# A transformer block on one core: an earlier start, reordered products and moved small work in the attention turns

## Chip, cores and metric

The kernel runs on 1 core of one Trainium2 chip. The metric is the device time of one execution in microseconds. Before the change it is 1411.21 us, the median of 3 runs (1409.51 to 1415.54).

## What is computed

Eight sequences of 512 tokens and 256 features, 16 heads of 16, go through two residual blocks. Everything is float32. Cut to its core, with `ln` for a layer norm without weights and `rn` for an RMS norm:

```python
def attn_block(x):                       # first block, applied to ln(x)
    q, k, v = split(x @ Wqkv_w.T + Wqkv_b)
    ctx = causal_attn(q, k, v)
    q2 = conv1d(ctx, conv_w, width=3, padding=1) + conv_b
    ctx2 = causal_attn(q2, k, v)         # the same k and v again
    return ctx2 @ out_w.T + out_b

def ffn_block(x):                        # second block, applied to ln(x)
    h = x + causal_attn_rotary(rn(x) @ wq, rn(x) @ wk, rn(x) @ wv) @ wo
    t = rn(h)
    w = top2_of_softmax(t @ w_router)    # 8 experts, two per token, weights scaled to sum 1
    return h + sum_over_experts(w * ((silu(t @ wg) * (t @ wu)) @ wd))

x = x + attn_block(ln(x))
x = x + ffn_block(ln(x))
```

So each sequence needs three causal attentions: one with q, one with q2, one with rotary q and k.

## The kernel before

**Two stages.** The first some 870 us are the attentions of all eight sequences and all that lies between them. Then come the experts, which gather their tokens from a table in DRAM (`xtab`) and are a plain row of matmuls. A sequence is a `Batch`; sequences go in pairs, and `one` and `two` are the pair at work, `before0` and `before1` the pair before it, `next0` and `next1` the next. The three attentions of a pair alternate between its two members.

**Steps and turns.** An attention of one sequence is 9 steps. A step computes, for one or two blocks of 64 keys, scores in two PSUM buffers `sc` (L1290) and an exponential out of each (L1297, ScalarE). GpSimd then masks the diagonal (L1305). The products with V (L1220) follow some steps later. A turn is two steps, a pair of sequences takes 27 turns, and there are 108 turns in all. Turn t+2 below is the third turn of a pair of sequences: turns 29, 56 and 83 for the second to fourth pair (turns 0 to 4 have a list of their own). In the profile turn 29 begins at 239.11 us and turn 30 at 248.09 us. The loop at the end of the kernel writes out each turn in this order:

1. first scores and their two exponentials
2. products with V of earlier steps (`catch_up`)
3. follow-ups listed as "mid"
4. `small_units[n]`, then `first_units[n]`
5. second scores and their two exponentials
6. follow-ups "late", then `units[n]`, then follow-ups "end"

Units are all other work of a sequence: projections, transposes, norms, routing. `plan(turn, batch, what, ...)` puts a unit into `units`, or into the list named with `among`. The block runs under `manual_schedule`, so PE, ScalarE, VectorE and GpSimd each execute their instructions in the order in which the program writes them. SP sends most DMAs.

**Resources.** `mm_tile()` hands out two PSUM banks in turn; a product that takes a bank waits until whoever read the product before last from that bank is done. The scores have two buffers, so a step's scores wait for the exponentials of the step before.

**Lines that the change and the prediction touch.**
- `load_x` (L746): one DMA of 512 KB for a sequence. `wqkv_sb` (L927) and `bqk_sb` (L944) are the QKV weights and the column of q and k biases. `bk_sb` (L1043) needs that column and `parity`.
- `stats` (L1385): mean and variance of each of four token chunks on VectorE (L1113, L1114), plus epsilon (L1391), power of -1/2 on GpSimd (L1392). `normed` (L1397) applies them (L1400). `transpose` turns the result by PE (L1372) and copies it out of PSUM on VectorE or ScalarE (L1376). `q`, `k`, `values` are projections (L1130, L1148) with their copies (L1436 q, L1419 k, L1166 values).
- `table_inputs` and `table`: the rotary tables, turned by PE (L1095) and copied by ScalarE (L1097), once.
- `normalise` (called when the products with V of half an attention are complete) copies sums out of PSUM (L1237, ScalarE), moves them by DMA (`r`, `cs`), and lists `finish` (L1250, L1251, VectorE) and `then`, which is `differences` in the first attention (four VectorE operations, L1471 to L1474) for the later `conv`.
- `bias`: one GpSimd addition to x for a chunk. `x1`: the residual after the first block and the norms behind it.
- `route`: some 25 small VectorE operations and one ScalarE exponential (L1675 to L1692). `slots`: two small products (L1706, L1707), some 20 small VectorE operations, then indirect DMAs from GpSimd (L1730) sent one by one in later turns.
- `h` (L1616 on): the output projection of the rotary attention for half of the tokens (PE L1119), the sum (VectorE L1622), the sum into x (GpSimd L1623), and the squares (ScalarE L1625), whose element-wise output goes back into the PSUM bank and whose row sums are what is used. `rms` follows both halves: L1632 (VectorE), L1633 (GpSimd), L1636 (VectorE).

At the start the program does 34 transposes of the identity into PSUM (L1906), whose result nobody reads.

Of the kernel before, what the change touches and what calls it, by code (L numbers as in the profile page):

```python
# [11 lines left out]
F32 = mybir.dt.float32  # L12
I32 = mybir.dt.int32
AF = mybir.ActivationFunctionType
# [677 lines left out]
def fast_path(  # L692
# [52 lines left out]

    def load_x(b):  # L746
        if b < B:
            xs[b] = keep.tile([P, NC, D], F32, tag="x", name="x", bufs=4)
            nc.sync.dma_start(xs[b], x[b * S : (b + 1) * S, :].rearrange("(c p) d -> p c d", p=P))

# [11 lines left out]

    load_x(0)

# [157 lines left out]
    with ExitStack() as att:  # L922
# [31 lines left out]
        for i in range(1, 3):  # L954
            va.append(wp.tile([P, NB, PAIRS, HP], F32, tag=f"va{i}", name=f"va{i}"))

        wqkv_sb = weight(wqkvT, 3 * D, "wqkv_sb")
        bqk_sb = column(bqkv[: 2 * D], 2 * D, "bqk_sb")
        nc.gpsimd.dma_start(bv_sb, bqkv[2 * D :].partition_broadcast(P))
# [52 lines left out]
        for i, n in enumerate((N, 2 * N, CAP + N)):  # L1012
# [25 lines left out]
            turns, ident.rearrange("p (f i) -> p i f", i=2), AX.X, ALU.add  # L1038
        )

        bk_sb = wp.tile([P, DC, 2], F32, tag="bk", name="bk_sb")
        for ch in range(DC):
            nc.vector.tensor_scalar(  # L1043
                bk_sb[:, ch, :], parity, bqk_sb[:, DC + ch : DC + ch + 1], None, ALU.mult
            )

# [157 lines left out]
        def attention(qT, kT, v, to, then=None):  # L1204
# [25 lines left out]
            def normalise(ch):  # L1230
# [28 lines left out]
                if then is not None:  # L1259
                    follow(1 - ch, lambda: then(ch), where)  # L1260
                follow(3 - 2 * ch, check, "late")
# [71 lines left out]
        class Batch:  # L1333
# [50 lines left out]

            def stats(self):  # L1385
                self.xb = xs.pop(self.b)
                mv = self.mv = small.tile([P, NC, 2], F32, tag="mv", name="mv")
                for c in range(NC):
                    moments(mv, self.xb, c)
                rstd = self.rstd = small.tile([P, NC], F32, tag="rstd", name="rstd")  # L1390
                nc.vector.tensor_scalar(rstd, mv[:, :, 1], LN_EPS, None, ALU.add)  # L1391
                nc.gpsimd.tensor_tensor(rstd, rstd, neghalf[:, 0, :], ALU.pow)  # L1392

            def fetch_next(self):
                load_x(self.b + 1)

            def normed(self):  # L1397
                xn = self.xn = self.normed_tile("xn")
                for c in range(NC):
                    nc.vector.tensor_scalar(  # L1400
                        xn[:, c, :],
                        self.xb[:, c, :],
                        self.mv[:, c, 0:1],
                        self.rstd[:, c : c + 1],
                        ALU.subtract,
                        ALU.mult,
                    )
                self.xT = self.tile([P, DC, S], "xT", "xT")

# [206 lines left out]
            def h(self, half):  # L1616
                if half == 0:
                    self.ss = small.tile([P, NC], F32, tag="ss", name="ss")
                two = slice(2 * half, 2 * half + 2)
                ps = self.project_two(self.c3, wo_sb, half)  # L1620
                h = self.rows[:, two, :D]
                nc.vector.tensor_add(h, h, ps)  # L1622
                nc.gpsimd.tensor_tensor(self.xb[:, two, :], self.xb[:, two, :], h, ALU.add)  # L1623
                for c in range(2 * half, 2 * half + 2):
                    nc.scalar.activation(  # L1625
                        ps[:, c - 2 * half], self.rows[:, c, :D], AF.Square, accum_out=self.ss[:, c : c + 1]
                    )
# [145 lines left out]
        for p in range(B // 2 + 1):  # L1773
# [5 lines left out]
            plan(t, before0, "transpose3", (0, True), (1, True))  # L1779
            plan(t, two, "q", 0)  # L1780
            plan(t, before0, "logits")
# [4 lines left out]
            plan(t + 1, before1, "normed2", 2, 3)  # L1786
            plan(t + 2, before1, "h", 0, 1)
            plan(t + 2, before1, "rms")
            plan(t + 3, two, "q", 1, among=first_units)
            plan(t + 3, two, "k", 1)  # L1790
            plan(t + 3, before0, "slots")
            plan(t + 3, next0, "fetch_next")
# [15 lines left out]
            plan(t + 11, next0, "k", 0)  # L1808
            for c in range(NC):
# [88 lines left out]
        with tc.manual_schedule(  # L1898
# [224 lines left out]
```

## Time and profile before

| what | value |
|---|---|
| median of the runs | 1411.21 us |
| profiled execution, its time | 1413.67 us |
| its span, first to last instruction | 1411.9 us |
| VectorE, ScalarE, GpSimd busy | 52%, 51%, 37% of the span |
| mean granted PE clock | 0.994 |
| exponentials (L1297) | 432 of 1023 ns |
| a projection matmul of q or k (L1130, 128x512) | 624 ns |
| load of x, 512 KB, from issue to landing | 4.3 us |
| load of the QKV weights, 768 KB | 6.1 us |
| load of the bias column, 2 KB | 7.5 us |

PE is TensorE's matmuls, PEld its weight loads, DVE VectorE, ACT ScalarE, POOL GpSimd, SP the engine that issues DMAs. In an order of time, a line gives the start and the length in us, the engine, the line of the program, the operation, what it writes and reads, and how many instructions were merged. A bracket gives the idle time of the engine before it and who ended it.

### The profile page before, as it was taken

Reading aid. Unit: us, or ns where it says so; the run is one execution under the profiler, and the core shown is the slowest. Engines: PE = TensorE matmul, PEld = TensorE weight load, DVE = VectorE, ACT = ScalarE, POOL = GpSimd, SP = SyncE. Lnnn points to the kernel's source line nnn. Section 1 sums busy time; section 2 is a strip of 40 time slices with the busy share of each in tenths; the row PEclk is TensorE's granted clock in tenths of the full one; section 3 lists DMA queues with packets and bytes.
Section 4 is the critical chain, followed back from the end, with each engine's and each line's share of the span. In section 5 each row is a group of like instructions: output and inputs, shape, how many; then the busy total and the mean of one; then the engine's idle time right before and its main releaser. Section 6 shows DMA issues by size and latency. Waiting matters only on the chain.

```text
span 1411.9 us, 31919 instructions
## 1 busy us (share of the span) xinstructions
PE 1369.0 (97%) x13476; PEld 892.3 (63%) x13476; DVE 739.6 (52%) x1470; ACT 723.6 (51%) x1175; POOL 525.2 (37%) x525
## 2 busy tenths in 40 slices
PE   8999999999999899999999999999999999999997
PEld 5566555566555566556565566666767677776775
DVE  5754886775887665886666865322222212222221
ACT  4677777776786677777776784321111211111120
POOL 3334434547333546433555444232122121222212
PEclk9999999999999999999999999999999999999998
DMA  5122122211001211011222022334141323232311
GB/s 151 59 82 86 66 82 77 73 40 62 13 25 53 73 40 55 20 45 39 83 72 79 21 84 71 90 81 102 23 102 31 96 32 95 46 87 42 88 26 14
DMA packets 66408, 88.42 MB, mean 63 GB/s; under 512 B 12752, under 2 KB 46736, under 8 KB 66256
## 3 DMA queue, kind: packets, MB, share of 16 engines
q1 hardware_dynamic: 52976, 68.94, 14.7%
q0 software_dynamic: 13280, 17.35, 7.0%
q8 instruction: 107, 1.75, 0.5%
q14 instruction: 45, 0.37, 0.1%
HBM read 36.35 MB, written 31.82 MB: 48 GB/s over the span
## 4 chain that ended last, share of the span: by engine, by line
PE 59%; DVE 5%; ACT 4%; DMA 1%; issue 1%; POOL 1%; DVEq 0%; POOLq 0%; ACTq 0%; SPq 0%
PE pgu L835 23%; PE po L860 13%; PE sc L1290 8%; PE av L1220 5%; PE mm L1130 3%; ACT pr L1297 2%; PE mm L1483 2%; PE mm L1119 1%; PE mm L1148 1%; PE mm L824 1%; DVE r L1250 1%; DVE c L1251 1%; PE mm L1372 1%; DMA r<-cs 1%; DMA cs<-cs 0%
## 5 line engine op out<-in xcount | busy, mean ns | idle before, releaser
L1297 ACT ACTIVATE pr<-sc 128x1024 f32<-128x1024 f32 x432 | 418.8, 1023 | 145.1 <-PE sc L1290 144.6
L1305 POOL TENSOR_TENSOR pr<-pr,seen 128x512 f32<-128x512 f32 (+1 forms) x216 | 256.6, 1188 | 395.7 <-ACT pr L1297 386.2
L835 PE MATMUL pgu<-xgT,gu 128*128 128x384 f32 (+1 forms) x1056 | 337.0, 478 | 1.9 <-DVE hT L850 1.6
L835 PEld LDWEIGHTS pgu<-xgT,gu 128*128 128x128 f32 x1056 | 200.4, 190 | 128.3 <-DVE hT L850 2.2
L849 ACT ACTIVATE sg<-pgu 128x384 f32<-128x384 f32 (+1 forms) x120 | 57.7, 481 | 404.5 <-PE pgu L835 404.4
L872 POOL DMA_INDIRECT out_dram<-share,xg x72 | 111.0, 1542 | 373.8 <-DVE share L867 299.6
L1220 PE MATMUL av<-pr,va 64*32 64x512 f32 (+7 forms) x6144 | 216.3, 407 | 0.0
L1290 PE MATMUL sc<-qT,kT 32*128 32x320 f32 (+7 forms) x2048 | 192.2, 436 | 4.3 <-ACT pr L1297 4.2
L850 DVE TENSOR_TENSOR hT<-sg,pgu 128x384 f32<-128x384 f32 (+1 forms) x120 | 65.0, 543 | 240.3 <-ACT sg L849 240.3
L860 PE MATMUL po<-dn,hT 128*128 128x256 f32 (+1 forms) x864 | 190.8, 379 | 0.0
L1220 PEld LDWEIGHTS av<-pr,va 64*32 64x32 f32 x6144 | 112.1, 106 | 101.2 <-issue 73.5
L860 PEld LDWEIGHTS po<-dn,hT 128*128 128x128 f32 (+1 forms) x864 | 159.9, 187 | 23.9
L1250 DVE RECIPROCAL r<-r 128x256 f32<-128x256 f32 x96 | 167.4, 1744 | 11.8 <-DMA r<-cs 11.7
L1290 PEld LDWEIGHTS sc<-qT,kT 32*128 32x128 f32 x2048 | 115.7, 185 | 78.3 <-ACT pr L1297 32.0
L867 DVE TENSOR_SCALAR share<-po,xg 128x256 f32<-128x256 f32 (+1 forms) x72 | 34.8, 483 | 148.6 <-PE po L860 148.5
L1290 PE MATMUL sc<-q2T,kT 32*128 32x512 f32 (+7 forms) x1024 | 93.0, 434 | 0.6 <-ACT pr L1297 0.5
L1730 POOL DMA_INDIRECT xtab<-rows,slot x64 | 64.0, 1000 | 46.0 <-DVE pick L1719 29.0
L1290 PEld LDWEIGHTS sc<-q2T,kT 32*128 32x128 f32 x1024 | 58.3, 184 | 32.7 <-issue 14.5
L1130 PE MATMUL mm<-xT,wqkv_sb 128*128 128x512 f32 x128 | 63.7, 624 | 3.9 <-ACT mm L1625 2.3
L1130 PE MATMUL mm<-xaT,wqkv_sb 128*128 128x512 f32 x128 | 61.3, 612 | 2.0 <-DVE xaT L1378 2.0
L1483 PE MATMUL mm<-terms,conv_sb 128*128 128x256 f32 x256 | 62.7, 390 | 0.0
L1237 ACT ACTIVATE cs<-av 128x512 f32<-128x512 f32 x96 | 56.6, 604 | 3.7 <-PE av L1220 3.2
(181 smaller groups left out, 1305.5 us busy)
## 6 DMA issues: line engine op xcount, KB each, us to landing
r<-cs SPq DMA_DIRECT2D x96, 128.0 KB, 2.0
xtab<-pad SPq DMA_DIRECT2D x24, 397.5 KB, 3.3
xg<-xtab SPq DMA_DIRECT2D x16, 397.5 KB, 3.0
gu<-in_wg_dram SPq DMA_DIRECT2D x18, 352.0 KB, 3.1
cs<-cs SPq DMA_DIRECT2D x48, 128.0 KB, 2.0
dn<-in_wd_dram SPq DMA_DIRECT2D x9, 640.0 KB, 5.1
gu<-in_wu_dram SPq DMA_DIRECT2D x18, 320.0 KB, 3.8
x<-in_x_dram SPq DMA_DIRECT2D x8, 512.0 KB, 4.3
```

The costliest lines, as they stand in the source:

```text
L835: nc.tensor.matmul(ps, gu[d][:, n0 : n0 + P], xgT[:, d, :], start=(d == 0), stop=(d == DC - 1),)
L850: nc.vector.tensor_mul(hT[k], sg, pu)
L860: nc.tensor.matmul(po, hT[k][:, s * P : s * P + m], dn[:, k, :], start=(k == 0), stop=(k == NK - 1),)
L872: nc.gpsimd.indirect_dma_start(out=out, out_offset=token_of(xg, s, m), in_=share[:m, s, :], in_offset=None, bounds_check=B * S - 1, oob_is ...
L1130: nc.tensor.matmul(ps, w[:, d, n0 : n0 + P], srcT[:, d, :S], start=(d == 0), stop=(d == DC - 1),)
L1220: nc.tensor.matmul(av[i][g * HP : (g + 1) * HP, j * KB :], v[rows, j, ch * G + g, :], pr[rows, g, at : at + n], start=(j == 0), stop=(j == ...
L1250: nc.vector.reciprocal(r[:, half], r[:, half])
L1290: nc.tensor.matmul(sc[:, g - g0, at : at + S - j * KB], kT[r0 : r0 + HP, ch, j], qT[r0 : r0 + HP, ch, j * KB : S], start=True, stop=True,)
L1297: nc.scalar.activation(pr[:, g0 : g0 + 2], sc, AF.Exp, scale=SCALE)
L1305: nc.gpsimd.tensor_tensor(diag, diag, seen.unsqueeze(1).unsqueeze(1).to_broadcast([P, G, len(parts), KB]), ALU.mult,).ins
L1483: nc.tensor.matmul(ps[:, i], conv_sb[:, d, k, ch * P : (ch + 1) * P], self.terms[d][:, k], start=(d == 0), stop=(d == DC - 1),)
L1730: nc.gpsimd.indirect_dma_start(out=xtab, out_offset=bass.IndirectOffsetOnAxis(ap=slot[:, c, k : k + 1], axis=0), in_=rows[:, c, :], in_off ...
```

## The change

- The first sequence's x is loaded as two DMAs; its moments, power and normalisation go by halves. The bias column is loaded ahead of the QKV weights, and `bk_sb` is computed behind the normalisation instead of ahead of it. The first sequence's transposes go by halves of the tokens, with one copy on ScalarE and one on VectorE. 22 transposes of the identity instead of 34.
- `then` (the differences) always goes to the "end" list.
- The squares in `h` are written to an SBUF tile (`t1`, which two other places also use) instead of the PSUM bank.
- `q` of `two` in turn t, the first half of `h` of `before1` in turn t+2, `slots` of `before0` in turn t+3, and `next1`'s transposes in turn t+25 go from `units` to `first_units`, ahead of the turn's second scores.
- The bias additions go to turns 6, 8, 10, 11 (`one`) and 10, 11, 15, 15 (`two`), instead of 10 to 13 and 14 to 17.
- The four rotary `table` units go from turns 3, 3, 4, 4 (`units`) to turns 2, 3, 4, 5 (`small_units`).

```diff
-    def load_x(b):
+    def load_x(b, parts=1):
...
-            nc.sync.dma_start(xs[b], x[b * S : (b + 1) * S, :].rearrange("(c p) d -> p c d", p=P))
+            of = x[b * S : (b + 1) * S, :].rearrange("(c p) d -> p c d", p=P)
+            n = NC // parts
+            for c in range(0, NC, n):
+                nc.sync.dma_start(xs[b][:, c : c + n, :], of[:, c : c + n, :])
...
-    load_x(0)
+    load_x(0, 2)
...
+        bqk_sb = column(bqkv[: 2 * D], 2 * D, "bqk_sb")
         wqkv_sb = weight(wqkvT, 3 * D, "wqkv_sb")
-        bqk_sb = column(bqkv[: 2 * D], 2 * D, "bqk_sb")
...
-        for ch in range(DC):
-            nc.vector.tensor_scalar(
-                bk_sb[:, ch, :], parity, bqk_sb[:, DC + ch : DC + ch + 1], None, ALU.mult
-            )
+        def bias_by_parity():
+            for ch in range(DC):
+                nc.vector.tensor_scalar(
+                    bk_sb[:, ch, :], parity, bqk_sb[:, DC + ch : DC + ch + 1], None, ALU.mult
+                )
...
                 if then is not None:
-                    follow(1 - ch, lambda: then(ch), where)
+                    follow(1 - ch, lambda: then(ch), "end")
...
+            def transpose_halves(self):
+                ps = [mm_tile() for _ in range(DC)]
+                for half in range(2):
+                    for d in range(DC):
+                        for c in range(2 * half, 2 * half + 2):
+                            nc.tensor.transpose(
+                                ps[d][:, c * P : (c + 1) * P],
+                                self.xn[:, c, d * P : (d + 1) * P],
+                                ident,
+                            )
+                for d in range(DC):
+                    (nc.scalar.copy, nc.vector.tensor_copy)[d](self.xT[:, d, :S], ps[d])
...
+                squares = small.tile([P, S], F32, tag="t1", name="t1", bufs=2)
                 for c in range(2 * half, 2 * half + 2):
                     nc.scalar.activation(
-                        ps[:, c - 2 * half], self.rows[:, c, :D], AF.Square, accum_out=self.ss[:, c : c + 1]
+                        squares[:, :D], self.rows[:, c, :D], AF.Square, accum_out=self.ss[:, c : c + 1]
                     )
...
-            plan(t, two, "q", 0)
+            plan(t, two, "q", 0, among=first_units)
...
-            plan(t + 2, before1, "h", 0, 1)
+            plan(t + 2, before1, "h", 0, among=first_units)
+            plan(t + 2, before1, "h", 1)
...
-            plan(t + 3, before0, "slots")
+            plan(t + 3, before0, "slots", among=first_units)
...
-            for c in range(NC):
-                plan(t + 10 + c, one, "bias", c)
-                plan(t + 14 + c, two, "bias", c)
+            for c, n in enumerate((6, 8, 10, 11)):
+                plan(t + n, one, "bias", c)
+            for c, n in enumerate((10, 11, 15, 15)):
+                plan(t + n, two, "bias", c)
...
-                plan(t + 25, next1, "transpose", (0, True), (1, True))
+                plan(t + 25, next1, "transpose", (0, True), (1, True), among=first_units)
...
-            units[3 + n // 2].append(lambda n=n: table(n))
+            small_units[2 + n].append(lambda n=n: table(n))
...
-                for i in range(17):
+                for i in range(11):
...
-            one.stats()
-            one.normed()
+            one.stats(0, 2)
+            one.stats(2, 2)
+            one.normed(0, 2)
+            one.normed(2, 2)
+            bias_by_parity()
+            one.transpose_halves()
             two.stats()
-            one.transpose(0)
-            one.transpose(1)
```

`stats(first, n)` and `normed(first, n)` do what they did, for n chunks from the first on.

More of the change, by code (lines that the diff above doesn't have):

```diff
@@ L1382, in transposed, with stats, normed @@
                     nc.scalar.mul(to[:, d, :S], ps, scale[:, d : d + 1])
-            def stats(self):
-                self.xb = xs.pop(self.b)
-                mv = self.mv = small.tile([P, NC, 2], F32, tag="mv", name="mv")
-                for c in range(NC):
[L1389 to L1392, printed above, removed]
+            def stats(self, first=0, n=NC):
+                if first == 0:
+                    self.xb = xs.pop(self.b)
+                    self.mv = small.tile([P, NC, 2], F32, tag="mv", name="mv")
+                    self.rstd = small.tile([P, NC], F32, tag="rstd", name="rstd")
+                some = slice(first, first + n)
+                for c in range(first, first + n):
+                    moments(self.mv, self.xb, c)
+                rstd = self.rstd[:, some]
+                nc.vector.tensor_scalar(rstd, self.mv[:, some, 1], LN_EPS, None, ALU.add)
+                nc.gpsimd.tensor_tensor(rstd, rstd, neghalf[:, 0, some], ALU.pow)
             def fetch_next(self):
                 load_x(self.b + 1)
-            def normed(self):
-                xn = self.xn = self.normed_tile("xn")
-                for c in range(NC):
+            def normed(self, first=0, n=NC):
+                if first == 0:
+                    self.xn = self.normed_tile("xn")
+                    self.xT = self.tile([P, DC, S], "xT", "xT")
+                xn = self.xn
+                for c in range(first, first + n):
                     nc.vector.tensor_scalar(
@@ L1407, in normed @@
                     )
-                self.xT = self.tile([P, DC, S], "xT", "xT")
+            def transpose_halves(self):
[10 more added lines that the diff above has]
+                    (nc.scalar.copy, nc.vector.tensor_copy)[d](self.xT[:, d, :S], ps[d])
             def transpose(self, d, soon=False):
@@ L1808, in fast_path @@
             plan(t + 11, next0, "k", 0)
-            for c in range(NC):
-                plan(t + 10 + c, one, "bias", c)
-                plan(t + 14 + c, two, "bias", c)
+            for c, n in enumerate((6, 8, 10, 11)):
+                plan(t + n, one, "bias", c)
+            for c, n in enumerate((10, 11, 15, 15)):
+                plan(t + n, two, "bias", c)
             plan(t + 12, two, "conv", (0, 0), among=first_units)
```

## The prediction

> **What bounds the kernel now.** I read the page first, then PE's waits, then the order of time on single engines around the places that the diff touches. Times below are those of the profiled execution (span 1411.9 us, run 1413.67 us, 2.5 us above the median of 1411.21 us).
>
> ```profile
> PE 1369.0 (97%) x13476; PEld 892.3 (63%) x13476; DVE 739.6 (52%) x1470; ACT 723.6 (51%) x1175; POOL 525.2 (37%) x525
> PE 59%; DVE 5%; ACT 4%; DMA 1%; issue 1%; POOL 1%; DVEq 0%; POOLq 0%; ACTq 0%; SPq 0%
> ```
>
> PE works 97% of the span, and the change takes no matmul away except 12 warm-up transposes. All it can win is PE's idle time, and only before 870 us: the experts behind that are PE without gaps. PE's waits (us in total, times, longest):
>
> ```profile
> PE sc L1290 <- ACT pr L1297: 4.7, 9, 0.9
> PE mm L1372 <- DVE va L1166: 4.5, 2, 2.8
> PE mm L1130 <- ACT mm L1625: 2.3, 3, 0.9
> PE mm L1095 <- ACT kT L1419: 1.3, 1, 1.3
> PE mm L1095 <- DVE va L1166: 1.2, 1, 1.2
> ```
>
> Each is a place that the diff edits: scores that wait for an exponential, transposes that wait for a PSUM bank which VectorE or ScalarE still reads. One of them costs more than its length. Here are windows of 1 us after the 2.85 us gap of turn 59 (columns: PE, PEld, DVE, ACT, POOL busy, clock, DMA share, GB/s):
>
> ```profile
> 478.00:479.00 1.00, 0.00 (x0) 0.00 (x0) 1.00 (x3) 1.00 (x4) 0.93 (x1) 1.00 0.00 0
> 479.00:480.00 1.00, 0.12 (x1) 0.15 (x2) 0.72 (x2) 0.13 (x2) 0.84 (x2) 0.51 0.28 109
> 484.00:485.00 1.00, 1.00 (x2) 0.48 (x3) 0.91 (x3) 1.00 (x2) 0.00 (x0) 0.50 0.00 0
> 486.00:487.00 1.00, 1.00 (x6) 0.29 (x8) 0.96 (x2) 0.18 (x1) 0.95 (x1) 1.00 0.00 0
> ```
>
> The granted clock fell to half from about 479.5 to 485.6. The same work (transposes to the next values) took 487.80 - 479.88 = 7.92 us here and 274.69 - 269.37 = 5.32 us in turn 32, so the gap cost 2.85 + 2.6.
>
> **The start.** PE's first useful work was released by this chain on VectorE:
>
> ```profile
> 5.20 0.43 DVE L1113 BATCH_NORM_STATS2 st<-x 128x6 f32<-128x256 f32 x1 [2.13 <-DMA x<-in_x_dram]
> 7.46 0.17 DVE L1391 TENSOR_SCALAR rstd<-mv 128x4 f32<-128x4 f32 x1
> 9.46 0.36 DVE L1043 TENSOR_SCALAR bk_sb<-parity,bqk_sb 128x2 f32<-128x2 f32 x2 [1.45 <-DMA bqk_sb<-in_bqkv_dram]
> 9.73 1.38 DVE L1400 TENSOR_SCALAR xn<-x,mv,rstd 128x256 f32<-128x256 f32 x4
> 12.16 0.43 DVE L1113 BATCH_NORM_STATS2 st<-x 128x6 f32<-128x256 f32 x1 [1.05 <-DMA x<-in_x_dram]
> ```
>
> The pow (POOL, 7.71 to 8.76) was done 0.7 us before the bias column, behind which the normalisation was queued. The change takes the column off that path and halves the chain. Say the first half of x lands at 4.1 to 5.1 (no half load is in the trace; the whole needs 4.3 us from issue): moments 2 x 0.57 each half, pow 1.05, second normalisation ends at 8.4 to 9.4, and the first projection, which came 1.05 us behind it, at 9.5 to 10.5 instead of 12.16. SP issues one DMA more ahead of the QKV weights (0.5 us); they landed at 7.4, so 8.4 with the column ahead of them, still early. But the second batch's x still lands at about 12.1; its moments stand ahead of q's bias on VectorE and end at 14.6, the bias takes 0.75, and the first scores need it: 15.45 instead of 17.69. That caps the gain at **-2.2**, which I take (ends -2.6 and 0; with a first projection at 10.5 it is -1.6).
>
> Fewer warm-up transposes: the trace shows 8 to 9 of them per us until 8.0 us and 14 per us after it, so full rate came 5.3 us after the first. 22 at about 0.22 us end at 7.5, as the first real transposes come. If full rate is then late by some 3 us, that eats the gain: the end 0 above. The Trainium skill ("TensorE: Matmul & The Clock Gate", "What's actually happening") says that warm-up is a budget of about 3.4 us of time, not a number of matmuls. By it 4.9 us of transposes are enough and the gain stays; by the trace's 5.3 us they are just short.
>
> **Rotary tables one by one, and earlier.** The 1.32 us at 49.52 (bank read by kT's bias) and 1.22 us at 58.94 (bank read by va's copy) go: between values and second scores each table finds its bank free (kT done at 34.85, va at 42.66) and its inputs ready (36.76, 45.9). **-2.5**; -2.0 if a ScalarE copy of 0.37 delays an exponential.
>
> **Turn 25 (three times): transposes ahead of the second scores.** Values end at 211.08; the scores wait 0.86 and, their second half waiting too, run to 213.98; transposes 1.09; then 0.35 for VectorE's copies. After: transposes to 212.2 (VectorE was idle 4.78 us there, the bank is free at 209.9), scores of 1.2 to 1.4 us, h(1) with nothing to wait for: 215.4 instead of 217.34 at its end, -1.9 each, **-5.7** (-3.6 if only the printed waits go).
>
> **Turn 0 (27, 54, 81): q ahead.** The second scores shrink by 0.4, but logits then stands directly behind its two transposes and needs both VectorE copies (0.41, then 0.34 more). **0** (ends -1, +1).
>
> **Turn 2 (29, 56, 83): h(0) ahead of the second scores.** This is the step that decides. The gain is a hidden wait of the scores (2.23 us from 242.21 to 244.44, against 1.2). The loss is on ScalarE, whose order is the written one. What ScalarE and VectorE do there now:
>
> ```profile
> 243.71 1.94 ACT L1297 ACTIVATE pr<-sc 128x1024 f32<-128x1024 f32 x2 [0.26 <-PE sc L1290]
> 249.49 0.39 ACT L1625 ACTIVATE mm<-rows 128x256 f32<-128x256 f32 x1 [3.84 <-DVE rows L1622]
> 248.77 1.27 DVE L1622 TENSOR_TENSOR rows<-rows,mm 128x512 f32<-128x512 f32 x2
> ```
>
> h's sum stands on VectorE behind the whole of `route`, which is still listed ahead of it (small work comes first), and starts at 248.77 although PE had finished h(0) by 246.3. Its squares wait for it, 3.84 us of idle ScalarE, and today only the next turn's exponentials are behind them. After the change h(0)'s squares are issued **before** the second scores' two exponentials. So: PE does h(0) to 244.1, second scores to 245.3, h(1) to 247.1; the next turn's scores need a buffer that those exponentials free; the sum ends at 249.4, two squares at 250.44, the first exponential at 251.4. PE stands idle for 4.3 us. With VectorE's chain 0.4 shorter (one link took 0.61 instead of 0.19 beside a GpSimd mask which now comes later) it is 3.9 us, longer than the 2.85 us that halved the clock.
>
> Behind it, at half clock by the rows of turn 59: scores to 253.4, values 1.2, q(two,1) 2.98 (1.98 at full clock; its wait of 0.69 for the squares is gone, since they now write SBUF), slots 0.6, second scores 1.2, k(two,1) 1.9: the next turn at 261.3 instead of 256.70, or 260.9 with the shorter chain. **+4.2 each, +12.6.** At full clock the same line gives +3.2 (k then waits for q's bias, behind the row scaling that needs h(1)'s squares and the pow): the lower end, 9.6. The upper end is 6.6 each: the full-clock line without the shortening, 3.6, plus half of the 6.1 us of half clock.
>
> The rule of that page says a wait of one idle window, about 3.4 us, halves the clock and 3.4 us of work restores it. By it a gap of 3.9 us costs 1.7 us of half-rate work beside it, by the row of turn 59 up to 3; and by it a 2.85 us gap should have cost no clock, where the trace shows that it did. The row decides; the rule, too, speaks against this step.
>
> **Turn 3: slots ahead.** Same work, 0.45 us earlier; nothing waits. 0.
>
> **Differences at the end of the turn.** In turns 32 and 59 the transposes waited 1.60 and 2.85 us for va's copies, queued on VectorE behind four differences (1.4 us). These now come behind, and PE arrives some 4 us later anyway: both waits go, with the half clock: -1.6 - 5.45 = **-7.0** (-4.0 if 1.4 us is all that each gains).
>
> **Bias adds moved on GpSimd.** 0.7 to 0.9 us each, two together in turns 10, 11 and 15; PE waits for GpSimd once, for the identity. 0; +1 if x1's pow comes late behind the two of turn 15.
>
> **Sum:** -2.2 - 2.5 - 5.7 + 0 + 12.6 - 7.0 = -4.8 on 1413.67: **1409 us**, 2 under the median. All terms at their good ends give 1404, all at their bad ends 1426.
>
> **Rivals.**
> 1. *ScalarE isn't held up* (the sum comes early, or the exponentials aren't behind the squares). Then turns 29, 56 and 83 gain 1.0 + 0.69 + 0.75 (the next second scores, 1.99 against 1.2) = 2.4 each: -2.2 - 2.5 - 5.7 - 7.3 - 7.0 = -24.7, **1389**. For it: ScalarE is busy 51%. Against: in turn 24 ScalarE did squares at 209.92 and the exponentials behind them at 210.88, while PE waited 0.86 us.
> 2. *The clock gate takes more than the waits* (slower). At the upper end, 19.8 for the three gaps, and half clock at the start takes that gain: 19.8 - 2.5 - 5.7 - 7.0 = +4.6, **1418**. Against the median it decides from 4.2 us a gap: without the start's, the other gains are 15.2; 15.2 - 2.5 (profiled run over median), over 3. For it: the clock did fall after 2.85 us. Against: PE has waits behind the gap that absorb slow work.
> 3. *Part of it does nothing*: x's half lands no earlier and turn 25 keeps a hidden wait. 0 - 2.5 - 3.6 + 12.6 - 7.0 = -0.5, **1413**. Against: 4.78 us of idle VectorE there.
>
> **Chances.** Forecast 0.60, rivals 0.15, 0.17, 0.08. This kernel's runs lie within 0.4%, so 0.5% (7 us: 1404 to 1418) is what can be told from no change. Faster: rival 1 and the low edge of the forecast, 0.22; slower: half of rival 2 and what I overlook, 0.17; same 0.61. The forecast's own range is 1403 to 1416; with a part of rivals 1 and 2 it is 1398 to 1420.
>
> **What would show it.** In turns 29, 56 and 83 a wait of PE's first scores for an exponential, near 4 us, and a granted clock of 0.5 behind it; squares ahead of exponentials on ScalarE. No waits of L1095, none of transposes for va, none of products for squares. First scores near 15.5 us. The prediction is wrong if the exponentials in turn 29 start by 246 us, or if gaps show up at places that have none now.

## The result and the profile after

The changed kernel takes 1419.68 us (median of 17 runs, 1414.4 to 1424.58) beside 1410.1 us (17 runs, 1408.46 to 1416.25) of the kernel before. The ratio is 1.0057, 95% interval 1.0046 to 1.0068: some 8 us slower by the ratio and 9.6 us between the medians, where 2 us faster was forecast. The profiled execution took 1417.95 us, its span 1416.2.

The engines' busy times, from the page of the changed kernel (busy us, share of the span, instructions):

```profile
PE 1372.5 (97%) x13464; PEld 892.5 (63%) x13464; DVE 738.7 (52%) x1472; ACT 723.2 (51%) x1174; POOL 524.6 (37%) x526
```

PE is busy 3.5 us longer with 12 matmuls fewer: some of its work ran slower. Its waits (us in total, times, longest):

```profile
PE sc L1296 <- ACT pr L1303: 13.0, 7, 4.1
PE mm L1136 <- DMA wqkv_sb<-in_wqkvT_dram: 1.8, 1, 1.8
PE mm L1378 <- ACT sinT L1103: 1.4, 1, 1.4
```

The waits for va, for kT and for the squares, which the prediction listed, are gone, as foreseen. In their place are three long waits of scores for an exponential, a wait for the QKV weights, and one for a rotary table. The long ones are in turns 29, 56 and 83. Turn 29 in order of time on PE and ScalarE, then windows of 1 us behind the gap (the columns as in the prediction):

```profile
242.38 1.99 PE L1125 MATMUL mm<-wo_sb,c 128*128 128x256 f32 x8
...
247.99 3.10 PE L1296 MATMUL sc<-qT,kT 32*128 32x448 f32 x16 [3.62 <-ACT pr L1303]
252.06 3.10 PE L1136 MATMUL mm<-xT,wqkv_sb 128*128 128x512 f32 x4
...
258.46 1.38 PE L1296 MATMUL sc<-qT,kT 32*128 32x320 f32 x16
```

```profile
245.98 0.42 ACT L1652 ACTIVATE t<-rows 128x256 f32<-128x256 f32 x1 [5.62 <-DVE rows L1647]
...
246.94 1.92 ACT L1303 ACTIVATE pr<-sc 128x1024 f32<-128x1024 f32 x2
```

The sum that the squares wait for, on VectorE behind `route`:

```profile
245.26 1.28 DVE L1647 TENSOR_TENSOR rows<-rows,mm 128x512 f32<-128x512 f32 x2
```

And the windows:

```profile
247.00:248.00 1.00, 0.01 (x1) 0.01 (x1) 0.00 (x0) 1.00 (x3) 0.21 (x1) 0.75 0.00 0
248.00:249.00 1.00, 1.00 (x6) 0.60 (x8) 0.00 (x0) 1.00 (x2) 0.00 (x1) 0.50 0.00 0
...
255.00:256.00 1.00, 1.00 (x13) 0.86 (x15) 0.81 (x2) 0.00 (x0) 0.00 (x0) 1.00 0.59 118
```

This is the step that the prediction called decisive, as it was drawn there: a square waits 5.62 us for h's sum, the exponentials wait behind the squares, PE waits 3.62 us (4.12 and 3.67 in turns 56 and 83; 3.9 foreseen), and the clock is at half from 247.5 to 254.3. The gap is right. What the other moves gain is too small. And of the two signs of being wrong that the prediction named, the second came: waits at places that had none, for the weights and for the table.

**By turns.** I took the time from the first scores of each turn to those of the next in the two profiled executions. After minus before, in us, and what the prediction had for the place:

| place | measured in the profiles | predicted |
|---|---|---|
| first scores of all | -1.07 | -2.2 |
| turns 2 and 3, 4, 5: tables | -1.4 - 1.4 + 2.0 = -0.8 | -2.5 |
| turns 25, 52, 79 | -1.45, -1.45, -1.43 | -1.9 each |
| turns 29 and 30 (56, 57; 83, 84): h and slots | +4.5, +4.6, +5.7 | +4.2 each |
| turns 32, 59: differences | -1.6, -5.7 | -1.6 - 5.45 |
| turns 7, 34, 61, 87: pauses of PE inside the products with V | +0.3, +0.5, +0.5, +0.7 | 0 |

One profiled execution is one draw, though, and what the two rows of the differences are worth in most executions is a question that this table can't answer. The experiments do.

### The profile page after: what moved, and what is told of

It reads as the page before. It is cut to its first block, busy times and chain, and to the rows that moved or that the text cites. A ratio compares the mean times of both kernels' runs of the same rounds, so it can differ in the third digit from the quotient of the medians.

```text
span 1416.2 us, 31897 instructions
## 1 busy us (share of the span) xinstructions
PE 1372.5 (97%) x13464; PEld 892.5 (63%) x13464; DVE 738.7 (52%) x1472; ACT 723.2 (51%) x1174; POOL 524.6 (37%) x526
## 5 line engine op out<-in xcount | busy, mean ns | idle before, releaser
L1226 PE MATMUL av<-pr,va 64*32 64x64 f32 (+7 forms) x6144 | 220.5, 409 | 0.0
L1296 PE MATMUL sc<-qT,kT 32*128 32x512 f32 (+7 forms) x2048 | 191.4, 439 | 12.8 <-ACT pr L1303 12.5
```

The lines of the kernel that those rows point to most:

```text
L1226: nc.tensor.matmul(av[i][g * HP : (g + 1) * HP, j * KB :], v[rows, j, ch * G + g, :], pr[rows, g, at : at + n], start=(j == 0), stop=(j == ...
L1296: nc.tensor.matmul(sc[:, g - g0, at : at + S - j * KB], kT[r0 : r0 + HP, ch, j], qT[r0 : r0 + HP, ch, j * KB : S], start=True, stop=True,)
```

## Experiments

Four chips were used: 11 for e1 to e4, 2 for e5 to e8, 7 for e9 to e12, 1 for e13 to e18. Every ratio below compares with runs of the kernel before on the same chip, whose medians are 1409.6 to 1412.5 us, so ratios and not times are to be compared; a difference of ratios is turned into us with 1410.

### A square: h(0) and slots

Four kernels, the changed one among them, with h(0) ahead or back and the slots ahead or back. e2 is h(0) ahead alone in the kernel before.

```diff
e1, e5 (from the changed kernel):
-            plan(t + 2, before1, "h", 0, among=first_units)
-            plan(t + 2, before1, "h", 1)
+            plan(t + 2, before1, "h", 0, 1)
e5, e11 (from the changed kernel):
-            plan(t + 3, before0, "slots", among=first_units)
+            plan(t + 3, before0, "slots")
e2 (from the kernel before):
-            plan(t + 2, before1, "h", 0, 1)
+            plan(t + 2, before1, "h", 0, among=first_units)
+            plan(t + 2, before1, "h", 1)
```

e1, h back. Expected:

> The changed kernel with both halves of h behind the second scores again. Theory 1 (ScalarE's order: h(0)'s squares ahead of the second scores' exponentials make the next turn's first scores wait, 4.5 to 5.7 us for each of three pairs): 14.9 us go, up to 1.7 come back because PE reaches turns 32 and 59 earlier and meets va's copies there; 1406 us (1403 to 1409), no first scores of turns 30, 57, 84 that wait over 1 us. Theory 2 (the loss sits in the other moves: start, tables, slots, bias, bank order): 1415 to 1420.

e2, h(0) ahead alone. Expected:

> The kernel before with h(0) ahead of the second scores and nothing else. Theory 1: 14.9 us come, and the waits of turns 32 and 59 for va (1.6 and 2.85 us) go, since PE is late there: 1420 us (1416 to 1423), a wait of some 3.6 us and a granted clock of 0.5 behind it in turns 30, 57 and 84. Theory 2: 1410 us, within 3.

e5, both back. Expected:

> The changed kernel with h and slots behind the second scores again (q, transposes, tables, differences, bias and start as changed). Theory: with slots ahead, k(two,1) gets the bank of q(two,1) and waits for q's bias, which stands on VectorE behind rms's row scaling; that wait and the half clock behind it cost 2.6, 4.0 and 2.8 us in turns 30, 57 and 84 of the run with h alone put back (1409.0). So 1400 us (1398 to 1403), k without a wait for qT. Rival (k's wait is only moved time, PE waits later instead): 1407 to 1410.

e11, slots back. Expected:

> The changed kernel with the slots' products alone back at their old place, h(0) still ahead with its squares. With both at hand (1419.7), h back (1409.0) and both back (1406.9) the fourth cell of a square. Theory that the slots' cost is a wait of k's products for q's bias on VectorE, which stands behind the scaling of the rows, wherever h stands: the gap of some 4 us and its half clock stay in turns 29, 56 and 83, turns 30 and 31 lose some 2 to 3 us a place: 1412 to 1414. Rival that the half clock behind the gap makes up most of the cost and the slots ahead only move it: 1418 to 1420.

| | slots ahead | slots back |
|---|---|---|
| h(0) ahead | 1419.68, ratio 1.0057 [1.0046, 1.0068] | e11: 1418.98, 1.0042 [1.0025, 1.0060] |
| h back | e1: 1408.98, 0.9972 [0.9954, 0.9991] | e5: 1406.91, 0.9962 [0.9945, 0.9979] |

e2: 1425.23 us, 1.0080 [1.0049, 1.0111]. So h(0) ahead costs 0.0085 with the slots ahead and 0.0080 without, 12.0 and 11.3 us, and 11.3 us alone. My 12.6 stands as a sum. The slots ahead cost 0.0010 or 0.0015, 1.4 to 2.1 us, within the noise of these four numbers; in e11 my expectation of 1412 to 1414 fell to its rival, and e5 came out at its rival's edge, not at 1400. What the slots do when no gap covers them is seen in e1 (PE, then VectorE, turn 30):

```profile
250.62 1.98 PE L1136 MATMUL mm<-xT,wqkv_sb 128*128 128x512 f32 x4
252.44 0.30 PE L1733 MATMUL mm<-both,before 128*128 128x32 f32 x2
...
256.68 3.50 PE L1136 MATMUL mm<-xT,wqkv_sb 128*128 128x512 f32 x4 [1.39 <-DVE qT L1461]
```

```profile
253.81 2.15 DVE L1663 TENSOR_SCALAR rows<-rows,ss 128x256 f32<-128x256 f32 x4 [1.13 <-POOL ss L1660]
255.88 0.74 DVE L1461 TENSOR_SCALAR qT<-mm,bqk_sb 128x512 f32<-128x512 f32 x1
```

There are two PSUM banks in turn. With the slots' product between q and k, k gets the bank of q, and has to wait until q's bias has been added, which stands on VectorE behind the scaling of the rows. Four products took 3.50 us behind this wait and 1.98 us ahead of it. In e5 the same places show no such wait. "Same work, nothing waits" was wrong as to mechanism. In time it was wrong by little here; where h(0) is ahead and its gap is gone it is 8.5 us (e3 against e6, below).

### The gap: its cause and its clock

```diff
e3 (from the changed kernel): h(0)'s squares behind the second scores' exponentials
-            plan(t + 2, before1, "h", 0, among=first_units)
+            plan(t + 2, before1, "h", (0, True), among=first_units)
...
+                if later:
+                    follow(0, square, "late")
e4 (from the changed kernel): h(1)'s products done three times, work in the gap
+                for i in [0, 1] * again:
+                    project(ps[:, i], self.c3, 2 * half + i, wo_sb, 0, D)
e6: e3 with the slots back
```

e4 does the eight products of h(1) twice more into the same bank.

> The changed kernel, h(0)'s product and sum still ahead of the second scores, its squares behind the second scores' exponentials. Theory 1: the wait goes and the second scores' hidden wait of 1 us a pair stays won: 1404 us (1401 to 1407). A rival to it (h(0)'s early product costs by its PSUM bank or by VectorE's order, not by ScalarE's): 1412 to 1420, with the wait of turns 30, 57 and 84 still above 2 us.

> The changed kernel with h(1)'s four products in turns 29, 56 and 83 executed three times, which fills the 3.6 us in which PE waits for ScalarE without making anything later. If the half clock behind the gap has a price of its own: the granted clock stays 1.0 there, first scores of turn 29 to first scores of turn 31 take 20.6 us instead of 22.1, in all -4.5 us, 1415 us. If PE's later waits (q's bias behind the row scaling) absorb slow work: 1419.7, within 1.5.

> The same, but h(0)'s product and sum stay ahead of the second scores and its squares come behind their exponentials. Theory: the second scores' hidden wait of 1 us a pair is won on top: 3 us less than with h and slots put back, 1398 us (1395 to 1400). Rival: nothing won, since the next turn's exponentials wait for the squares all the same: the same time as with h and slots put back, within 1.

e3: 1412.45 us, 1.0000 [0.9981, 1.0018]. The gap is gone: the second exponentials of turn 29 start at 243.84, ahead of the squares (ScalarE, below; in the changed kernel at 246.94, behind them), and the first scores of turn 30 do not wait, where they waited 3.62 us. So ScalarE's order makes the gap.

```profile
243.84 1.94 ACT L1303 ACTIVATE pr<-sc 128x1024 f32<-128x1024 f32 x2 [2.19 <-PE sc L1296]
247.25 0.42 ACT L1653 ACTIVATE t<-rows 128x256 f32<-128x256 f32 x1 [1.47 <-DVE rows L1647]
```

That 1404 did not come is the slots' doing: e6, which differs from e3 in nothing else, is 0.0060 faster. k now arrives early and waits longer, with half the clock behind it (PE):

```profile
247.55 1.98 PE L1136 MATMUL mm<-xT,wqkv_sb 128*128 128x512 f32 x4
...
254.31 3.78 PE L1136 MATMUL mm<-xT,wqkv_sb 128*128 128x512 f32 x4 [2.05 <-DVE qT L1461]
```

e6, without the slots: 1405.03 us, 0.9940 [0.9916, 0.9964], not to be told from e5, where h stays back, so the 3 us more that I expected did not come: by turns h(0) ahead takes 1.0 us off turn 29 and gives 0.7 back in turn 30, even when nothing holds it up.

e4 is the plainest look at the clock: 1411.47 us, 0.9986 [0.9969, 1.0004]. With 16 needless products more in each of three turns it is 0.0071 or 10 us faster than the changed kernel, more than twice the 4.5 us that I expected. Turn 29 of e4, PE and windows:

```profile
244.92 5.45 PE L1125 MATMUL mm<-wo_sb,c 128*128 128x256 f32 x24
250.51 2.11 PE L1296 MATMUL sc<-qT,kT 32*128 32x448 f32 x16
...
253.14 1.98 PE L1136 MATMUL mm<-xT,wqkv_sb 128*128 128x512 f32 x4
...
255.42 1.17 PE L1296 MATMUL sc<-qT,kT 32*128 32x384 f32 x16
```

```profile
248.00:249.00 1.00, 1.00 (x6) 0.87 (x6) 0.46 (x1) 0.50 (x2) 0.46 (x1) 1.00 0.00 0
250.00:251.00 1.00, 0.85 (x5) 0.31 (x5) 0.60 (x1) 1.00 (x2) 0.00 (x0) 1.00 0.00 0
```

The needless work fills the time in which PE would stand, the clock stays at 1.00, and q takes 1.98 us instead of 3.10. Three stretches of 6.8 us at half clock are 3 x 3.4 = 10.2 us of lost work, about the 10 us that e4 gets back. e4 is still 0.0024, 3.4 us, above e5, which has neither gap nor moved slots. So most of what h(0) ahead costs is the clock behind the gap, not the gap itself.

The other executions fit. The mean granted clock of the changed kernel's 17 runs is 0.989, that of the 110 runs of the kernel before beside the experiments 0.995. One minus the clock, times the span, is 15.8 and 6.6 us of lost clock; the 9 us between them, an estimate, are as much as the whole loss. At full clock, by this estimate, the gaps and the gains of the change would about cancel.

### The other moves, one by one

With h and the slots back (e5) the rest of the change gains 0.0038, 5.4 us, where I had -17.4. So the fault had to be in the start, the tables, turn 25 or the differences.

```diff
e13 (from the kernel before): the changed start alone (loads, halves, 22 warm-up products)
e14 (from the kernel before):
-                    follow(1 - ch, lambda: then(ch), where)
+                    follow(1 - ch, lambda: then(ch), "end")
e15 (from the kernel before):
+                plan(t + 25, next1, "transpose", (0, True), (1, True), among=first_units)
+            small_units[2 + n].append(lambda n=n: table(n))
```

> The kernel before with the changed start alone: x in two loads, the bias column ahead of the weights, 22 warm-up products, moments and normalisation by halves, transposes by halves. My prediction's term: -2.2 us, so ratio 0.9984. Theory that the weights land later behind the split loads and the column, and the short warm-up then loses the clock: between 0 and +2.5 us in the mean, ratio 1.000 to 1.002, first scores anywhere from 16.6 to 20.5 us.

> The kernel before with one word changed: what follows a finished row of scores (the differences) is hung at the end of the turn for both halves, not in its middle for the first. My prediction's term: -7.0 us (3.5 each in turns 32 and 59), ratio 0.9950; by turns the changed kernel shows -6.7. Theory that this term is right: -6.5 to -7. If the 0.5 us pauses of turns 8, 34, 61 and 88 come from it, they appear here and the gain is -5; if they don't, they come from another part.

> The kernel before with the rotary tables one a turn in turns 2 to 5 and the transposes of turns 25, 52 and 79 ahead of the second scores, and nothing else. My prediction's terms: -2.5 and -5.7, so -8.2 us, ratio 0.9942. By the turns of the changed kernel: tables -0.8 (the transposes of turn 5 wait 1.4 us for the last table's copy on ScalarE), turn 25 -4.35, so -5.2, ratio 0.9963.

| run | measured | ratio | in us | predicted |
|---|---|---|---|---|
| e13, start | 1411.13 | 1.0002 [0.9983, 1.0022] | +0.3 | -2.2 |
| e14, differences | 1406.69 | 0.9973 [0.9955, 0.9992] | -3.8 | -7.0 |
| e15, tables and turn 25 | 1404.86 | 0.9958 [0.9940, 0.9976] | -5.9 | -8.2 |

e13 also shows why the differences had to disappoint. It leaves turns 32 and 59 as they were. The same place of turn 59, VectorE's first product with the reciprocal and PE's transposes that wait for va; before's VectorE and PE first, then e13's:

```profile
474.42 0.43 DVE L1251 TENSOR_TENSOR cx<-cs,r 128x256 f32<-128x256 f32 x1 [1.36 <-DMA cs<-cs]
```

```profile
479.88 1.94 PE L1372 MATMUL mm<-ident,xn 128*128 128x128 f32 x8 [2.85 <-DVE va L1166]
```

```profile
473.21 0.43 DVE L1257 TENSOR_TENSOR cx<-cs,r 128x256 f32<-128x256 f32 x1
```

```profile
478.70 1.07 PE L1378 MATMUL mm<-ident,xn 128*128 128x128 f32 x8 [1.60 <-DVE va L1172]
```

In before's execution VectorE waited 1.36 us for a DMA, PE's wait grew to 2.85 us, and the clock fell to half. In e13's it did not wait, PE waited 1.60 us as in turn 32, and the clock stayed: the same turn is 4.07 us shorter without a change to it. e2 shows that step too, while e15 has the long wait of PE (2.73 us) again, with VectorE waiting 1.21 us at the same place. In e14 VectorE waits 1.42 us there, but va's copies no longer stand behind the differences: PE waits 1.43 us, the clock stays, and the turn is 3.39 us shorter than in before's profile. So where the DMA is late the move does what I said, and it is late in three of these five profiles (before, e14, e15). The 5.45 us that I saw go was in some executions and not in others. Before's profiled execution was one of those with much half clock: its mean granted clock is 0.994, and 81 of the 110 later ones had more.

**The start.** e13's weights come late, and so do those of the changed kernel and of e17 (below), each time issued behind x's second half and the column (PE; first e13, then e17):

```profile
7.49 1.43 PE L1427 MATMUL mm<-ident,xn 128*128 128x128 f32 x8 [0.76 <-DVE xn L1412]
10.95 3.67 PE L1136 MATMUL mm<-xT,wqkv_sb 128*128 128x512 f32 x8 [2.03 <-DMA wqkv_sb<-in_wqkvT_dram]
```

```profile
7.43 1.22 PE L1427 MATMUL mm<-ident,xn 128*128 128x128 f32 x8
12.45 6.44 PE L1136 MATMUL mm<-xT,wqkv_sb 128*128 128x512 f32 x8 [3.80 <-DMA wqkv_sb<-in_wqkvT_dram]
```

The transposes are 2.8 us earlier than before's (10.28), as intended, and the weights, which had landed with time to spare, are now what PE waits for. In e17 the wait brings the half clock (11.2 to 18.0 us): eight products take 6.44 us instead of 3.67. First scores in the ten profiles with the changed start came at 16.1 to 20.7 us, 18.4 in the mean (e6, e13 and the changed kernel first, e5, e1 and e17 last); in the seven with the start of before at 16.6 to 17.8 us, 17.1 in the mean. In seven of the ten the clock fell to half for 3.4 or 6.8 us before 20 us, in none of the seven. No run has the changed loads with 34 warm-up products, so what the late weights and what the shorter warm-up does to the clock can't be told apart. e17's profiled execution was the slowest of its five (1403.26 us).

### The start: four tries at its weights

```diff
e7 (from e6): weights ahead of the column, the column's products behind the transposes,
              the second sequence's moments behind the values
e8 (from the changed kernel): start of before, but the column's products ahead of the moments on VectorE
e9 (from e6): start of before as it was
e10 (from e6):
-            nc.sync.dma_start(t, src.rearrange("(c p) n -> p c n", p=P))
+            nc.scalar.dma_start(t, src.rearrange("(c p) n -> p c n", p=P))
              and table 3 in turn 6 instead of 5, the column's products behind the transposes
```

> As the run before, with the start mended: QKV weights loaded ahead of the bias column, the column's products behind the transposes' copy, the second batch's moments behind q's bias and va's copy. Theory: the 2 KB column ahead of the weights is what made them land at 10.8 to 12.7 us instead of 7.4; here they land by 8.5, the first projection starts by 10.0, no half clock behind it, first scores by 15.7 instead of 16.6 to 20.5: 3 us less, 1395 us (1392 to 1398). Rival (the two halves of x and their order in the queue delay the weights): first projection at 10.8 or later, time as before it.

> The changed kernel with the start of before (one load of x, weights ahead of the column, 34 warm-up transposes, column's products first, whole moments). First scores were at 16.6, 18.1, 19.2 and 20.5 us in four profiles with the changed start and at 17.3 and 17.7 with the old one. Theory: the changed start loses more often than it gains, by the half clock: 1418.5 us (1416.5 to 1419.5). Rival (it gains what the one profile of the changed kernel shows, 1.1 us): 1420.8.

> The start alone, taken back from the version with the slots back and the squares late (1405.0 us, ratio 0.994): one load of x, the weights ahead of the bias column, 34 warm-up products, whole moments and normalisation, the column's products between them, as in the kernel before. Theory that the changed load order and the shorter warm-up cost time on most executions (first scores seen at 16.1, 16.6, 18.1, 19.2, 19.9 and 20.5 us against 17.3 and 17.7 with the old start): about 1404, between 1403 and 1405, and the first scores of the profile at 17.3 to 17.7 us with the weights' wait under 1 us. Rival that the changed start still gains the 2.2 us of my sum: 1407. A third, that it makes no difference in the mean: 1405.

> The same version (1405.0 us) with the QKV weights issued on ScalarE's queue, so not behind the halves of x and the column, the bias products behind the transposes' copies, and rotary table 3 made one turn later. Theory that the weights are late because they stand behind other loads in SyncE's queue: they land before 9.5 us, the first products wait less than 0.5 us for them, first scores at 15 to 16 us, and the 1.4 us wait of the transposes for ScalarE's table copy is gone: 1401 to 1402.5. Rival that the loads share the engines whoever issues them: weights' wait stays 1.3 to 4 us, and the time is 1404 to 1406.

e7: 1412.96 us, 0.9999 [0.9983, 1.0015]. The column isn't what holds the weights up, for they are late without it (PE waits 2.84 us). Nor is it x's bytes alone: the last packet of x starts at 3.9 us, and all but one of the weights' from 5.1 us on, where in before they start at 3.6 us. Why two halves of x hold the weights up more than x as a whole, no run shows. In e7 the moved moments held up turn 1 by 5.08 us besides. e8: 1422.11 us, 1.0077 [1.0050, 1.0105]. This is not the start of before: the column was there at 8.28 us and, now ahead of the moments, held all of VectorE up. It says nothing on the question. e9, with before's order: 1404.32 us, 0.9935 [0.9915, 0.9955], 0.7 us better than e6 and not to be told from it.

e10: 1404.96 us, 0.9947 [0.9930, 0.9964], no gain. On ScalarE's queue the weights' packets start at 2.4 us, and PE no longer waits for them. But x's second half reaches VectorE only at 8.80 us, where in before all of x was there at 5.20, and the first transposes wait for x's normalisation instead (PE, then VectorE):

```profile
2.68 4.52 PE L1944 MATMUL mm<-ident 128*128 128x128 f32 x22 [2.68 <-POOL ident masks.py:199]
11.03 1.99 PE L1427 MATMUL mm<-ident,xn 128*128 128x128 f32 x8 [3.82 <-DVE xn L1412]
```

```profile
8.80 0.43 DVE L1119 BATCH_NORM_STATS2 st<-x 128x6 f32<-128x256 f32 x1 [1.78 <-DMA x<-in_x_dram]
```

So x (512 KB) and the weights (768 KB) share what moves them: side by side, x is late. No order tried beats before's.

### The pauses, and the best version

e12 puts the bias additions back to see if they cause the pauses in turns 7, 34, 61 and 87:

```diff
e12 (from e6):
-            for c, n in enumerate((6, 8, 10, 11)):
+            for c, n in enumerate((10, 11, 12, 13)):
...
-            for c, n in enumerate((10, 11, 15, 15)):
+            for c, n in enumerate((14, 15, 16, 17)):
```

> The version of 1405.0 us with the eight bias additions back at their old turns. In the changed kernel TensorE stands still 0.5 us in the middle of the products with V in turns 8, 34 to 35, 61 to 62 and 88, where the kernel before does not. Theory that the moved additions cause it: the pauses go, and the time is 1403, some 2 us less. Rival that they have nothing to do with it: unchanged, 1404.5 to 1405.5, and the pauses stay at the same turns.

e12: 1405.69 us, 0.9943 [0.9922, 0.9964], the pauses still there (0.3 to 0.7 us). The bias additions are free either way, as predicted. The pause of turn 7 comes with the changed start, for e13 has it too. Those of turns 34, 61 and 87 go with the chip: all eight profiles on chips 2 and 7 (e5 to e12) have them, none of the ten on chips 11 and 1 (e1 to e4, e13 to e18) does. So they are not the change's doing as far as is known; what makes them, and whether the kernel before has them on those chips, no profile shows.

Last, what earned time together (e16), the same with the changed start (e17), and the changed kernel with the start of before (e18):

```diff
e16 (from the changed kernel): start of before, h and slots back, and
-            small_units[2 + n].append(lambda n=n: table(n))
+            small_units[(2, 3, 4, 6)[n]].append(lambda n=n: table(n))
e17 (from e16): the changed start
e18 (from the changed kernel): the start of before
```

> What earned time put together: the changed kernel with the start of before, h and the slots at their old turns, and table 3 one turn later. From the version with h and slots back (1406.9, ratio 0.9962): the old start gives some -1 to -2 us, the table 1.5: about 1404, ratio 0.994; by the turns of the profile (tables -2.3, turn 25 -4.35, differences -6.7, pauses +1.5) 1400, ratio 0.992. Rival that the late start was an accident of single executions: 1405.5.

> The version of 1397.3 us (ratio 0.9911) with the changed start instead of that of before (and h written plainly, which makes the same instructions). Theory that the changed start costs only 0.3 us, as alone: ratio 0.991 to 0.992, some 1398. Theory that it costs more beside the other moves (the weights' wait of up to 4 us and the half clock behind it in the profiles of five of them): ratio 0.994 to 0.995, 1401 to 1403. Rival that my -2.2 was right: 1395, ratio 0.9895.

> The changed kernel (1419.7, ratio 1.0057) with the start of before and nothing else. Theory that the start costs 0.3 us: 1419, ratio 1.005 to 1.006. Theory that it costs 4 us beside the other moves: 1415 to 1416, ratio 1.003. Rival that my -2.2 was right: 1422, ratio 1.007. The first scores of its profile at 16.8 to 17.8 us.

| run | us | ratio |
|---|---|---|
| e16 | 1397.29 (6 runs) | 0.9911 [0.9877, 0.9945] |
| e17 | 1398.65 (5 runs) | 0.9914 [0.9899, 0.9929] |
| e18 | 1416.57 (6 runs) | 1.0043 [1.0030, 1.0056] |

e16 beats both kernels: 0.9% or 12.5 us under the one before, 1.5% under the changed one. Its granted clock is 1.0 from 6.0 to 1388 us without a break (mean 0.998; 0.991 in the changed kernel). Turn 29 there has no wait, and the transposes ahead of the last table none either:

```profile
239.76 3.72 PE L1125 MATMUL mm<-wo_sb,c 128*128 128x256 f32 x16
243.41 1.22 PE L1296 MATMUL sc<-qT,kT 32*128 32x448 f32 x16
```

The changed start costs 0.4 us in e17 (0.0003) and 2.0 in the changed kernel (0.0014, against e18): 0 to 2 us, and no gain. The table one turn later is the one other change between e17 and e5, and their ratios differ by 0.0048, 6.8 us; but the two ran on different chips. By turns it is 1.5 us at the table itself and 1.6 at the pauses that go with the chip. The rest I can't place; the ends of the two intervals leave 2.3 to 11.3.

## Why the prediction was wrong

**Right: turn 29.** Mechanism, place and sum: squares on ScalarE ahead of the exponentials, a gap of 3.6 to 4.1 us (3.9 foreseen), 11.3 to 12.0 us in all (12.6 foreseen). The split was off, so that the sum came out is in part luck. I gave the clock 1 us a gap and the rest 3.2; e4 gives the clock 3.3 us a gap and, beside e5, leaves 1.1 for the rest. The Trainium skill ("TensorE: Matmul & The Clock Gate", "What's actually happening") has the clock fall after an idle window of some 3.4 us. In e1 it was at half from 256.3 to 259.8 us with no single wait of PE longer than 1.39 us around it, so the rows went against the rule as they did in turn 59.

**Wrong, and what decided: the sum of the gains,** -17.4 in the prediction, -5.4 in e5 and -9.4 as the sum of e13, e14 and e15. Tried alone, the differences fell short by 3.2 us, the start by 2.5, the tables and turn 25 by 2.3. By its steps:

- **Differences, "-1.6 - 5.45 = -7.0"**: measured -3.8 (-6.3 to -1.1), the low end that I named (-4.0). The step failed by taking the half clock of turn 59 for a property of the kernel. It comes where a DMA is late (1.36 us in before's profile), which is so in some executions and not in others. The profiled run, 2.5 us above the median, was a hint. The half clock was also 6.8 us long by the clock's records (479.0 to 485.8), not 6.1.
- **The start, "still early"** of the weights: measured +0.3 alone, +0.4 and +2.0 beside other moves. Behind two halves of x and the column the weights land later than my 8.4 us: PE waits 1.3 to 4.1 us for them in the ten profiles, and in seven of these the clock falls. The end 0 of my range was the right one, and not for the reason given: full clock came 2.8 to 5.9 us after the first warm-up product in the profiles of all 20 kernels, with 22 products as with 34. (The rates that I read there were wrong: 4.7 products a us until 8.0 us and 9.3 after it.)
- **Tables, "-2.5"**: by turns -0.8. I looked at banks and inputs, and not at who empties the bank after the last table: a ScalarE copy that stands behind exponentials and the sums of turn 5, on which the next transposes wait:

```profile
60.02 0.66 PE L1378 MATMUL mm<-ident,xn 128*128 128x128 f32 x4 [1.38 <-ACT sinT L1103]
```

- **Turn 25, "-1.9 each"**: -1.4 to -1.5 each by turns, between my two ends of -1.2 and -1.9. With the tables, -5.9 measured of -8.2.
- **Slots, "nothing waits. 0"**: +1.4 to +2.1, and +8.5 in e3. Moving a product that takes a bank turns the order of the two banks, so k met q's.
- **Bias additions, 0**: right (e12). **q ahead in turn 0, 0**: right by turns, not tried alone.

Done singly, the parts give 11.3 + 1.4 + 0.3 - 5.9 - 3.8 = +3.3 us; +8 was measured. Of the 4.7 between, the start's dearer place beside the other moves is 1.7; each single number has an interval of some 2.5 us either way, so what is left isn't shown to be anything. The pauses, 1.7 us in the profile without turn 7's, can't be booked for it, as they go with the chip.

Rival 2's 1418 is near the measured time, but not by its sum: the gaps cost 11.3 to 12.0 us and not 19.8, and the gains that it took over from the forecast did not come.

## What to carry to other kernels

In a kernel whose engine is 97% busy, price a gap by the work behind it at half clock, and look in more than one execution for whether a costly wait is always there before you book its going as a gain. When a product that takes one of two banks is moved past another, write down again who gets whose bank, and who empties it behind what. A transfer brought forward makes another late: list all that land in the same microseconds.

## What was not expected of the hardware

- Needless products made the kernel faster: 48 matmuls in three turns that change nothing gave 10 us back, because the clock did not fall.
- All stretches of half clock inside the profiled runs last 3.4 or 6.8 us, and in the changed kernel the stretches at full clock between the three gaps are 204.8 and 208.2 us, 60 and 61 times 3.41: the clock changes in steps of 3.41 us, whatever the length of the wait.
- Whether turn 59 pays 1.4 or 5.5 us hangs on whether VectorE waits 1.36 us for one DMA (e13 against before's profile).
